# Late outputs through two matmul banks and a last chunk in three parts, a unit of filler work in every step, and the recurrence's banks marked at the start

## The chip, the cores and the metric

One NeuronCore of a Trainium2 chip runs the whole program in one launch. Time is device time in microseconds (us). The engines are named as in the profile: PE (TensorE, matmuls), PEld (its weight loads), DVE (VectorE), ACT (ScalarE), POOL (GpSimd), SP (SyncE, which issues most transfers). Before: a median of 1362.26 us in 3 runs (1359.16 to 1363.05).

## The reference

The input x has 8 sequences of 512 positions and 256 channels, and there is a conditioning vector per sequence. Four residual layers follow each other, all in float32:

- layer 0: a shared gated MLP plus 8 experts, of which each position uses 2;
- layer 1: a wavelet transform, gated and inverted; since the gate is constant along the sequence, the kernel multiplies by a factor instead;
- layer 2: a low-rank adapter whose weights are made from the conditioning vector;
- layer 3: a gated recurrence over the 512 positions, with one output product per position.

```python
def step(H, xs):
    xz, xr, xh = xs
    Z = jax.nn.sigmoid(xz + H @ Whz.T + bhz)
    R = jax.nn.sigmoid(xr + H @ Whr.T + bhr)
    H_tilda = jnp.tanh(xh + R * H @ Whh.T + bhh)
    H_new = Z * H + (1.0 - Z) * H_tilda
    Y = H_new @ Whq.T + bhq
    return (H_new, Y)
```

The result is x plus the four residuals. The recurrence is strictly serial; layers 0 to 2 work on each position alone, so a window of positions can be prepared while earlier positions run through the recurrence.

## The kernel before

The sequence is cut into 16 windows of 32 positions (256 columns with the batch) for layers 0 to 2, and into 32 chunks of 16 positions for the recurrence. The program has three stages.

*Prologue.* Loads, the conditioning products, the routing of the first four windows, the generated adapter weights and the first windows of layers 0 to 2. The prologue uses its own matmul (PSUM) banks: `c` for small products, `gp` for generated adapter weights, `more` as a third bank for the hidden products of window 0. When the prologue's pools are closed, these banks pass to the recurrence.

*The loop.* 512 steps are written out one after the other (from line 1262 on). A step is: r and z products of the state (PE, line 1113), sigmoid (ACT, 1279), transposes (DVE, 1293), r times state (1310), the candidate's product (PE), tanh (ACT), transpose, and a scan that makes the new state (DVE, 1367). Then ACT copies the state into the chunk's history `hist` (1381). Input products and biases for later steps are put into gate banks ahead of time: `grh` (two buffers, r and candidate) and `gz` (z, both halves in one bank). The biases are written there by ACT, and the input and state products accumulate onto them, so each bank has to be marked once beforehand by matmuls that write all of it: `claim` (lines 1143 to 1149, called just before the loop; 12 matmuls of 512 columns).

*Filler work.* All other work is cut into jobs, held in queues per engine. One PE unit is four matmuls side by side (`quads`, line 413). `Jobs.fill` takes ready jobs at fixed places of a step, by the planner's own clock (2.43 us per step): on PE an early slot between the z products and the candidate's product, and a late slot behind the candidate's product. Each slot is asked for a number of units: the early one for 1 and the late one for 2 when `behind(s)` says that more units are left than a straight line down to step 462 allows, and both for none otherwise (or for 1 each once the queue is empty, `late(s)`). Within an engine the emitted order is the order of execution.

*Outputs.* At the end of each chunk `output_jobs` queues its four PE units (two halves of the channels by two of the contraction), two DVE operations that add the product, the bias and x in place (line 1202), and, where a block of positions is complete, the transfers out on SP (line 1214). Chunks 0 to 11 go to the urgent queue; chunks 12 to 31 are held in `jobs.last`, which is opened when PE's other queues are empty. All of them use one bank, `r_m` ("misc"), which holds both channel halves; the next chunk takes it when both DVE operations are done. After the loop `jobs.drain` emits what is left.

Of the kernel before, what the change touches and what calls it, by code (L numbers as in the profile page):

```python
# [9 lines left out]
F32 = mybir.dt.float32  # L10
# [6 lines left out]
P = 128  # L17
# [16 lines left out]
GS = 4  # L34
NG = TC // GS
TO = 64
HELD = 12
EPS_GATE = 1e-09
EPS_LN = 1e-05
# [26 lines left out]
class Ring:  # L66

    def __init__(self, pool, tag, shape, bufs):  # L70
        self.pool, self.tag, self.shape = pool, tag, shape
        self.held = [None] * bufs
        self.made = self.asked = 0

# [8 lines left out]
    def take(self, lazy):  # L83
        self.held[self.made % len(self.held)] = lazy
        self.made += 1
        return self.pool.tile(
            self.shape, F32, name=f"{self.tag}_{self.made}", tag=self.tag
        )
# [108 lines left out]
def cond_resid_kernel(  # L197
# [76 lines left out]
    r_mid = ring("mid", pair, 2)  # L274
    r_xt = ring("xt", [P, KC, WS, B], 3)

    jobs = Jobs()

    def load(out, in_, mb, lazies=(), deps=()):
# [35 lines left out]
    def load_x(n, mb):  # L315
# [21 lines left out]


    r_w2 = Ring(pro.enter_context(tc.tile_pool(name="w2q", bufs=5)), "w2", [P, R * C], 5)
    r_c, r_gp, r_more = (  # L340
        Ring(pro.enter_context(tc.tile_pool(name=n, bufs=b, space=PSUM)), n, shape, b)
        for n, shape, b in (("c", [P, 512], 1), ("gp", [P, 512], 1), ("more", pair, 1))
    )
    pieces = {}
    for pair_ in LOW:
        for k in range(KC):
# [63 lines left out]
    def quads(out, lhs, rhs, start, tiles=NQ):  # L410

        for j in range(tiles):
            nc.tensor.matmul(  # L413
                out[ts(j, 32)],
                lhs[:, ts(j, 32)],
                rhs,
                start=start,
                stop=False,
                skip_group_check=True,
            )  # L420
# [4 lines left out]
    def window_jobs(w, routed, xt, via_pool=False):  # L425
# [57 lines left out]
        def bank():  # L483

            turn[0] += 1
            return Lazy(r_more if w == 0 and turn[0] % 3 == 0 else r_h)

        def hidden(lazy, n, lhs, got):
            last = None
# [499 lines left out]
    for n, of in enumerate(LOW):  # L989
        pick = set1.tile([P, 2, R, B], F32, name=f"pick{n}")  # L990
        nc.vector.memset(pick, 0.0)
        for side, q in enumerate(of):
# [3 lines left out]
                .rearrange("p (r o) -> p r o", o=1)  # L996
                .broadcast_to([4 * R, R, B]),
            )
        gp = Lazy(r_gp)

        def biased_rows(gp=gp, pick=pick):
            quads(gp.get()[:, :C], pick.rearrange("p s r b -> p (s r b)"), b2, True)

        j = pe(biased_rows, [got_b2], [gp], 0.45)
        for k in range(KC):
            got = [pieces[q, k] for q in of]

            def generate(k=k, of=of, gp=gp):
                for r in range(R // 2):
                    for t in range(NQ):  # L1010
                        w = pieces[of[t // 2], k][0].get()
                        nc.tensor.matmul(
                            gp.get()[ts(t, 32), :C],
                            hid[:, r, k, :],
                            w[:, ts(R // 2 * (t % 2) + r, C)],
                            start=False,
                            stop=False,
                            skip_group_check=True,
                        )

            j = pe(
                generate,
                [j, got_hid, *(g[1] for g in got)],
                [gp, *(g[0] for g in got)],
                1.75,
            )
        j = got_low_out[n] = dve(
            lambda n=n, gp=gp: nc.vector.tensor_copy(low_out[:, n], gp.get()[:, :C]),
            [j],
            [gp],  # L1030
            0.45,
# [43 lines left out]
    with (  # L1075
        tc.tile_pool(name="gw", bufs=1) as gw,
        tc.tile_pool(name="gs", bufs=3) as gs,
        tc.tile_pool(name="ps_g", bufs=2, space=PSUM) as ps_g,
        tc.tile_pool(name="ps_z", bufs=1, space=PSUM) as ps_z,
    ):  # L1080
        brow = brows[0]
        tt(brow, brow, brows[1], ALU.add)
# [9 lines left out]
        for u in range(GS):  # L1092
# [6 lines left out]
            s = gw.tile([P, KC, B, 2], F32, name=f"d0_{u}")  # L1099
            nc.vector.memset(s, 0.0)  # L1100
            d0s.append(s)


        gz = ps_z.tile([P, 2, NG, FQ], F32, name="gz")

        def new_gates(c):
            rh = ps_g.tile([P, NG, 2, FQ], F32, name=f"grh_{c}", tag="grh")
            return rh, gz[:, c % 2]

        def across(out, lhs, rhs, start=False):  # L1110

# [29 lines left out]
                lambda: bias(z, brow[:, 1]),  # L1141
            ]

        def claim(banks):

            some = wsq_a[:, 0, 0:2].rearrange("p a (n f) -> p a n f", f=FQ)
            for out in banks:
                for j in range(NQ):
                    nc.tensor.matmul(
                        out[ts(j, 32)], ident[:, 0:32], some, start=True, stop=True  # L1150
                    )

        def project(g, gates):

            rh, z = gates
# [17 lines left out]
        def state(u):  # L1173
            return lambda k: s_h[u][:, k, :, :, 1]

        last_out = {}

        def output_jobs(c, hist, copied):
            queue = jobs.urgent if c < HELD else jobs.last
            ps = Lazy(r_m)  # L1180
            last = None
            for m in range(KC):
                for k in range(KC):
                    last = jobs.add(
                        "PE",
                        lambda m=m, k=k: quads(
                            ps.get()[:, m, : TC * B],
                            wh[:, k, G_Q, ts(m, P)],
                            hist[:, k].rearrange("p t b -> p b t"),
                            k == 0,  # L1190
                        ),
                        [last, copied],
                        [ps],
                        0.45,
                        queue,
                    )
            t0 = c * TC
            at, tile_x = [g for g in xg if g[0] <= t0][-1]

            def finish(m):  # L1200
                x = tile_x[:, m, :, t0 - at : t0 - at + TC]
                stt(
                    x,
                    ps.get()[:, m, : TC * B].rearrange("p (b t) -> p b t", t=TC),
                    vec[:, V_HQ, m : m + 1],
                    x,
                    ALU.add,
                    ALU.add,
                )

                t1 = t0 + TC
                n = TO if t1 <= T - TO else 2 * TC if t1 == T - 2 * TC else TC
                if t1 % n == 0 and (n < TO or t1 % TO == 0) and t1 != T - 3 * TC:
                    nc.sync.dma_start(
                        out=outs_[:, m, :, t1 - n : t1],
                        in_=tile_x[:, m, :, t1 - n - at : t1 - at],
                    )

            for m in range(KC):
                last_out[c] = jobs.add(  # L1220
                    "DVE", lambda m=m: finish(m), [last], [ps], 0.3, queue
                )

        both = [new_gates(c) for c in range(2)]
        claim([gz] + [g[0].rearrange("p n g f -> p g n f") for g in both])
        gates = both[0]
        for part in biases(gates):
            part()
# [33 lines left out]
        for c in range(NTC):  # L1262
            hist = hists[c]
            gates = upcoming
            for t in range(TC):
# [64 lines left out]

                ahead = s + 5
                part = None
                if c + 1 < NTC and t == 6:
                    upcoming = new_gates(c + 1) if c else both[1]
                    bias_parts = biases(upcoming)
# [17 lines left out]
                cand, act_c = gate(rh[:, n, 1], AF.Tanh, "c", KC)  # L1353
                if part is not None:
                    part()
                jobs.fill("PE", now + 1.44, 2 if behind(s) else 1 if late(s) else 0)
                if bias_parts and t >= 7:
                    biased.append(bias_parts.pop(0)())
                    if not bias_parts:
# [24 lines left out]
                    last_copy.done = at + 0.2  # L1384

                last_copy = Job("ACT", None, [], [])
            output_jobs(c, hist, last_copy)
        copying(base)
        jobs.drain(base + T * STEP)

# [64 lines left out]
```

## Time and profile before

| what | us |
|---|---|
| median of the runs | 1362.26 |
| profiled execution | 1358.07 |
| its span, first to last instruction | 1355.9 |
| first scan of the loop starts at | 78.95 |
| last scan of the loop starts at | 1338.25 |
| PE busy, DVE busy, ACT busy | 1179.3, 913.8, 503.7 |

A row in order of time gives the start, the length, the engine, the line, the operation, the tiles written and read, and how many instructions were merged (each float32 matmul appears as two rows). In brackets stands the engine's idle time before the row and what ended it. A line for a stretch gives, for each engine, the busy time and the number of instructions, then the clock that was granted to PE (1.00 is full), the share of the DMA engines and their rate. PE's busy time counts each matmul from its start to its modelled end, and matmuls overlap, so it is no measure of how much more would fit.

### The profile page before, as it was taken

The numbers are of one execution on the slowest core, as the hardware profiler recorded it, in microseconds if no ns is written. First come the engines' busy times: TensorE is split into PE (matmuls) and PEld (weight loads), VectorE is DVE, ScalarE is ACT, GpSimd is POOL, SyncE is SP. The second block draws the span as 40 slices with busy tenths as digits, with TensorE's granted clock in tenths as the row PEclk, the third lists the DMA queues.
The fourth block names the chain that finished last, engine by engine and source line by source line (L and its number), as shares of the span: only waits on it lengthen the run. The fifth ranks groups of instructions, "written<-read, shape, count | busy, mean of one in ns | idle before, by whom it ended". The sixth has DMA issues, their size and how long they took to land.

```text
span 1355.9 us, 89216 instructions
## 1 busy us (share of the span) xinstructions
PE 1179.3 (87%) x39380; PEld 722.5 (53%) x39380; DVE 913.8 (67%) x6248; ACT 503.7 (37%) x3402; POOL 137.4 (10%) x203
## 2 busy tenths in 40 slices
PE   7999998989898998988898888888888888878776
PEld 4555555555555555555455555555555555545443
DVE  4267777776776767676676766667676767666664
ACT  1133334343343434334343433434343343433331
POOL 0211010101011110101011010101101010110000
PEclk8999999999999999999999999999999999999999
DMA  9631001100101010100101010010101000000102
GB/s 348 208 126 35 5 5 36 52 5 5 36 20 35 5 35 4 42 14 5 35 4 35 4 35 4 4 35 4 35 4 35 4 5 4 5 4 5 34 20 33
DMA packets 47092, 46.48 MB, mean 34 GB/s; under 512 B 24064, under 2 KB 44000, under 8 KB 45296
## 3 DMA queue, kind: packets, MB, share of 16 engines
q1 hardware_dynamic: 46384, 38.65, 9.3%
q8 instruction: 307, 5.03, 1.5%
q0 software_dynamic: 320, 2.13, 0.4%
q14 instruction: 81, 0.66, 0.2%
HBM read 36.45 MB, written 4.33 MB: 30 GB/s over the span
## 4 chain that ended last, share of the span: by engine, by line
PE 73%; DVE 14%; ACT 7%; issue 4%; DMA 2%; SPq 1%; DVEq 0%; ACTq 0%
PE grh L1113 33%; PE hp L413 13%; PE acc L413 10%; DVE rT L1293 6%; PE misc L413 6%; PE gz L1113 5%; PE low L413 4%; ACT r L1279 4%; DVE d L1293 3%; DVE s_rh L1310 2%; ACT c L1279 2%; DVE s_h L1367 2%; DMA x<-in_xT_dram 1%; SPq L283 1%; DMA wh<-in_sq_b_dram 1%
## 5 line engine op out<-in xcount | busy, mean ns | idle before, releaser
L1113 PE MATMUL grh<-wh,s_h 128*32 128x64 f32 x8192 | 227.5, 226 | 103.6 <-DVE s_h L1367 100.9
L1293 DVE STREAM_TRANSPOSE rT<-r 128x32 f32<-128x32 f32 x1024 | 156.0, 190 | 233.1 <-ACT r L1279 230.2
L1279 ACT ACTIVATE r<-grh 128x32 f32<-128x32 f32 x1024 | 146.2, 195 | 445.3 <-PE grh L1113 442.9
L1113 PEld LDWEIGHTS grh<-wh,s_h 128*32 128x32 f32 x8192 | 145.8, 110 | 256.1 <-DVE s_h L1367 251.2
L1113 PE MATMUL grh<-wh,s_rh 128*32 128x64 f32 x8192 | 224.4, 226 | 49.2 <-DVE s_rh L1310 25.2
L1279 ACT ACTIVATE c<-grh 128x32 f32<-128x32 f32 x1024 | 146.3, 195 | 315.4 <-PE grh L1113 313.2
L1113 PEld LDWEIGHTS grh<-wh,s_rh 128*32 128x32 f32 x8192 | 141.7, 109 | 202.9 <-DVE s_rh L1310 197.5
L1293 DVE STREAM_TRANSPOSE d<-c 128x32 f32<-128x32 f32 x1024 | 156.6, 192 | 121.0 <-ACT c L1279 114.8
L1113 PE MATMUL gz<-wh,s_h 128*32 128x64 f32 x8192 | 212.7, 220 | 1.3 <-issue 1.2
L1113 PEld LDWEIGHTS gz<-wh,s_h 128*32 128x32 f32 x8192 | 156.2, 111 | 1.7 <-issue 1.6
L413 PE MATMUL hp<-x,sw_sb 128*32 128x256 f32 x2016 | 152.3, 388 | 2.3 <-ACT sig L509 1.0
L413 PE MATMUL hp<-x,rw_sb 128*32 128x256 f32 x2016 | 151.8, 383 | 1.4 <-ACT sig L541 0.6
L557 POOL TENSOR_TENSOR g<-gl,bc 128x256 f32<-128x256 f32 x128 | 93.8, 733 | 532.3 <-DVE s_h L1367 348.9
L1367 DVE TENSOR_TENSOR_SCAN s_h<-d,d 128x16 f32<-128x16 f32 x1024 | 145.3, 184 | 0.0
L413 PE MATMUL acc<-g,rw_sb 128*32 128x256 f32 x2048 | 144.4, 379 | 0.1
L1310 DVE TENSOR_TENSOR s_rh<-rT,s_h 128x8 f32<-128x8 f32 x1024 | 133.7, 168 | 0.0
L1293 DVE STREAM_TRANSPOSE zT<-z 128x64 f32<-128x64 f32 x512 | 121.9, 238 | 1.1 <-ACT z L1279 1.0
L1279 ACT ACTIVATE z<-gz 128x64 f32<-128x64 f32 x512 | 121.1, 237 | 1.9 <-PE gz L1113 1.5
L1113 PE MATMUL grh<-wx,xt 128*32 128x128 f32 x2048 | 108.7, 275 | 2.2 <-ACT r L1279 2.2
L1381 ACT COPY hist<-s_h 128x16 f32<-128x16 f32 x512 | 106.1, 207 | 0.5 <-DVE s_h L1367 0.5
L1322 DVE TENSOR_TENSOR d<-zT,s_h 128x16 f32<-128x16 f32 x512 | 90.5, 177 | 17.5
L1323 DVE TENSOR_SCALAR d<-zT 128x16 f32<-128x16 f32 x512 | 86.6, 169 | 0.0
(146 smaller groups left out, 1202.8 us busy)
## 6 DMA issues: line engine op xcount, KB each, us to landing
bc<-comb_d SPq DMA_DIRECT2D x56, 256.0 KB, 4.1
w<-in_w_dram SPq DMA_DIRECT2D x8, 1024.0 KB, 17.2
out_dram<-x SPq DMA_DIRECT2D x14, 256.0 KB, 3.1
x<-in_xT_dram SPq DMA_DIRECT2D x2, 1536.0 KB, 9.7
rw_sb<-in_rw_dram SPq DMA_DIRECT2D x2, 1024.0 KB, 13.3
bc<-comb_d POOLq DMA_DIRECT2D x2, 1024.0 KB, 10.8
sw_sb<-in_sw_dram SPq DMA_DIRECT2D x3, 512.0 KB, 5.5
wsq_a<-in_sq_a_dram SPq DMA_DIRECT2D x1, 1280.0 KB, 9.7
```

The costliest lines, as they stand in the source:

```text
L283: lambda: nc.sync.dma_start(out=out.get() if isinstance(out, Lazy) else out, in_=in_),
L413: nc.tensor.matmul(out[ts(j, 32)], lhs[:, ts(j, 32)], rhs, start=start, stop=False, skip_group_check=True,)
L557: lambda gl=gl, g=g, e=e: nc.gpsimd.tensor_tensor(g.get().rearrange("p (h t) -> p h t", t=P), gl.get().rearrange("p (h t) -> p h t", t=P), ...
L1113: nc.tensor.matmul(out[ts(j, 32)], lhs, rhs[:, ..., ts(j, FQ)], start=start, stop=False, skip_group_check=True,)
L1279: nc.scalar.activation(x, y, func)
L1293: ins = nc.vector.transpose(dst.rearrange("p i u b -> p i (u b)"), src.rearrange("p (i r) -> p i r", r=32),)
L1310: prod = tt(s_rh[u][:, k, u, :], rT[:, k, u, :], h[:, k], ALU.mult)
L1322: tt(d1[:, :, u, :, 1], zT[:, :, u, :], h, ALU.mult)
L1323: nc.vector.tensor_scalar(d0[:, :, :, 1], zT[:, :, u, :], -1.0, 1.0, ALU.mult, ALU.add)
L1367: new = nc.vector.tensor_tensor_scan(s_h[v][:, k, v].rearrange("p b w -> p (b w)"), d0[:, k].rearrange("p b w -> p (b w)"), d1[:, k, u].re ...
L1381: nc.scalar.copy(hist[:, :, t, :], s_h[v][:, :, v, :, 1])
```

## The change

- Held outputs (chunks 12 to 31) no longer use the one bank `r_m`: each channel half takes one of the two buffers of `r_h`, the banks of the hidden products, and each half's DVE operation depends on its own half alone.
- The last chunk's output is queued in three parts: its first 8 positions at step 7 of the chunk, the next 4 at step 11, the last 4 (`TAIL`) after the loop. Its very last transfer is issued by ACT instead of SP.
- The late slot is asked for 2 units when behind and for 1 otherwise, in every step.
- The gate banks are allocated at the outset. `gz` and the first `grh` buffer are marked before anything else on PE, by 8 matmuls of 256 columns each over a tile of zeros; the second `grh` buffer serves the prologue's small products (instead of `c`) and is marked in step 4 of the loop. `gp` and `more` are gone: the generated weights use `r_m`, and window 0's third bank is `r_low`.

```diff
+TAIL = 4
...
     def take(self, lazy):
         self.held[self.made % len(self.held)] = lazy
         self.made += 1
+        if self.given is not None:
+            return self.given
...
+    ps_g = pool_of("ps_g", 2, PSUM)
+    ps_z = pool_of("ps_z", 1, PSUM)
+    gz = ps_z.tile([P, 2, NG, FQ], F32, name="gz")
...
+    both = [new_gates(c) for c in range(2)]
+    zeros = const.tile([P, NT], F32, name="zeros")
+    nc.vector.memset(zeros, 0.0)
+    rh0, rh1 = [g[0].rearrange("p n g f -> p (n g f)") for g in both]
+
+    def claim(bank):
+
+        for half in range(2):
+            for j in range(NQ):
+                nc.tensor.matmul(
+                    bank[ts(j, 32), ts(half, NT)],
+                    zeros[:, 0:32],
+                    zeros,
+                    start=half == 0,
+                    stop=half == 1,
+                    skip_group_check=True,
+                )
+
+    claim(gz.rearrange("p c n f -> p (c n f)"))
+    claim(rh0)
...
+    r_c = Ring(None, "c", None, 1, rh1)
...
-            return Lazy(r_more if w == 0 and turn[0] % 3 == 0 else r_h)
+            return Lazy(r_low if w == 0 and turn[0] % 3 == 0 else r_h)
...
-        gp = Lazy(r_gp)
+        gp = Lazy(r_m)
...
-        def output_jobs(c, hist, copied):
-            queue = jobs.urgent if c < HELD else jobs.last
-            ps = Lazy(r_m)
-            last = None
+        def output_jobs(c, hist, copied, a=0, n=TC):
+
+            held = c >= HELD
+            queue = jobs.last if held else jobs.urgent
...
+                t1 = t0 + a + n
+                size = TO if t1 <= T - TO else 2 * TC if t1 == T - 2 * TC else TC
+                if t1 % size or (size < TO and t1 == T - 3 * TC):
+                    return
+                (nc.scalar if t1 == T and m else nc.sync).dma_start(
+                    out=outs_[:, m, :, t1 - size : t1],
+                    in_=tile_x[:, m, :, t1 - size - at : t1 - at],
+                )
+
+            ps = None if held else Lazy(r_m)
+            todo, last = [], None
             for m in range(KC):
+                if held:
+                    ps = Lazy(r_h)
+                half = 0 if held else m
...
+                    [j if held else last],
...
-        claim([gz] + [g[0].rearrange("p n g f -> p g n f") for g in both])
...
+                if c == 0 and t == 4:
+                    claim(rh1)
...
-                jobs.fill("PE", now + 1.44, 2 if behind(s) else 1 if late(s) else 0)
+                jobs.fill("PE", now + 1.44, 2 if behind(s) else 1)
...
-            output_jobs(c, hist, last_copy)
+                if c == NTC - 1 and t in (TC // 2 - 1, TC - TAIL - 1):
+                    a = 0 if t < TC // 2 else TC // 2
+                    output_jobs(c, hist, last_copy, a, t + 1 - a)
+            if c < NTC - 1:
+                output_jobs(c, hist, last_copy)
+        output_jobs(c, hist, last_copy, TC - TAIL, TAIL)
         copying(base)
         jobs.drain(base + T * STEP)
```

## The prediction

> **What bounds the kernel now.** I read the page first (span, chain), then the rows in order of time for the last 30 us, then stretches of the 512 steps, and last the first 76 us.
>
> ```profile
> span 1355.9 us, 89216 instructions
> PE 73%; DVE 14%; ACT 7%; issue 4%; DMA 2%; SPq 1%; DVEq 0%; ACTq 0%
> out_dram<-x SPq DMA_DIRECT2D x4, 64.0 KB, 2.5
> ```
>
> The chain is mostly PE, but it is a loop through PE, ACT and DVE. Rows in order of time show what one turn costs:
>
> ```profile
> 1328.58 0.28 DVE L1367 TENSOR_TENSOR_SCAN s_h<-d,d 128x16 f32<-128x16 f32 x2
> 1330.27 1.11 PE L413 MATMUL misc<-hist,wh 128*32 128x128 f32 x16
> 1331.00 0.28 DVE L1367 TENSOR_TENSOR_SCAN s_h<-d,d 128x16 f32<-128x16 f32 x2
> 1331.72 0.64 PE L413 MATMUL misc<-hist,wh 128*32 128x128 f32 x8
> 1332.69 0.65 PE L413 MATMUL misc<-hist,wh 128*32 128x128 f32 x8
> 1333.42 0.28 DVE L1367 TENSOR_TENSOR_SCAN s_h<-d,d 128x16 f32<-128x16 f32 x2
> 1335.83 0.28 DVE L1367 TENSOR_TENSOR_SCAN s_h<-d,d 128x16 f32<-128x16 f32 x2
> ```
>
> The columns are start, length, engine, line. One block unit is 8 matmul rows. Two units in the late slot (after the candidate's matmuls), one in each slot, and none at all: the scans stay 2.42 us apart. So the step is the loop's latency, and units cost nothing where they fit. From the first scan (78.95) to the last (1338.25) 511 steps take 1259.3 us; at 2.42 they would take 1236.6. The 22.7 us between are stalls. Of these 7.5 are waits of PE for nothing but issue (the waits of PE between 76 and 1339, "issue" rows added: 4.2 + 1.2 + 1.0 + 0.7 + 0.4). Another part is the clock:
>
> ```profile
> 513.10:516.52 3.42, 1.81 (x80) 1.21 (x80) 2.50 (x18) 1.88 (x11) 0.00 (x0) 1.00 0.02 5
> 516.52:519.93 3.41, 2.89 (x84) 2.39 (x88) 2.69 (x17) 0.90 (x7) 0.00 (x0) 0.50 0.02 7
> 516.45 0.28 DVE L1367 TENSOR_TENSOR_SCAN s_h<-d,d 128x16 f32<-128x16 f32 x2
> 519.32 0.28 DVE L1367 TENSOR_TENSOR_SCAN s_h<-d,d 128x16 f32<-128x16 f32 x2
> ```
>
> In the first two lines PE's busy time is the second number, the granted clock the last but two. After a stretch in which PE was busy 1.81 of 3.42 us the next 3.41 us ran at 0.50, and the steps in it took 2.87 and 2.63 instead of 2.42 (scans at 516.45, 519.32, 521.95): 0.66 lost. There are seven such stretches (from 352.68, 427.77, 516.52, 595.03, 752.04, 987.56, 1233.32); the steps in them lost 1.2, 1.0, 0.7, 1.0, 1.1, 1.2 and 0.5, together 6.7.
>
> The end:
>
> ```profile
> 1338.25 0.29 DVE L1367 TENSOR_TENSOR_SCAN s_h<-d,d 128x16 f32<-128x16 f32 x2
> 1339.64 0.61 DVE L1202 SCALAR_TENSOR_TENSOR x<-misc,vec,x 128x128 f32<-128x128 f32 x2 [1.10 <-PE misc L413]
> 1340.39 2.04 PE L413 MATMUL misc<-hist,wh 128*32 128x128 f32 x32 [0.82 <-DVE x L1202]
> 1351.19 0.61 DVE L1202 SCALAR_TENSOR_TENSOR x<-misc,vec,x 128x128 f32<-128x128 f32 x2 [2.26 <-PE misc L413]
> ```
>
> After the last scan five chunks' outputs go through one bank, 2.87 us each (matmuls, DVE, wait), and the span ends 17.4 us behind that scan (1338.54 to 1355.9). Last, the start of the loop:
>
> ```profile
> 2.56 0.99 PE L881 MATMUL c<-cond,inv_c 128*128 128x8 f32 x4 [2.56 <-DVE pick L991]
> 8.76 1.79 PE L763 MATMUL c<-rout,x 128*32 128x8 f32 x120 [1.30 <-DMA x<-in_xT_dram]
> 66.66 2.28 PE L1149 MATMUL grh<-wsq_a,ident 128*32 128x512 f32 x16
> 67.14 0.36 DVE L1082 TENSOR_TENSOR brow<-brow,brow 128x192 f32<-128x192 f32 x1 [0.99 <-DMA brow<-in_bias_rows_dram]
> 68.38 2.08 PE L413 MATMUL low<-mid,wsq_a 128*32 128x256 f32 x30
> 68.74 0.41 DVE L615 TENSOR_TENSOR u<-misc,own 64x256 f32<-64x256 f32 x1
> 70.32 1.00 PE L413 MATMUL low<-u,low_out 128*32 128x256 f32 x12
> ```
>
> **The change part by part**, priced against the profiled execution (1358.07 us, 2.2 of it around the span).
>
> *Tail.* The order as built has 80 output matmuls (20 units) behind the last step before, 16 narrow ones (4 units of 32 columns) after; from step 466 to 505 nearly every step now carries two. They fit: steps with two late units kept 2.42 above, and the one DVE finish per step (0.33) lies in DVE's 0.69 us between a scan's end and the next transpose (1328.86 to 1329.55). What remains behind the last scan: the history copy 0.03 + 0.21; four units, between 0.4 (31 matmuls of 8 columns took 0.44) and 2.05 (32 matmuls of 128 columns), I take 0.6, because with a quarter of the columns they lie nearer to the narrow row; two finishes between 0.17 and 0.33 each, 0.4; 2.5 from issue to landing of 64 KB; 1.2 from the last landing to the end, as now (issued 1352.2 + 2.5 = 1354.7, end 1355.9). With 0.1 for two handovers that is 5.0: **-12.4**. The second half's transfer is issued by ACT, which issues none before. Bounds: as SP's (2.5), and POOL's 5.1 to landing for 32 KB. Best case 4.6 (-12.8), worst 9.0 (-8.4).
>
> *Marks at the outset.* 16 matmuls of 256 columns (four units) now head PE's queue, behind a memset of 128x256 (0.28 on DVE). At the rates of that time (1.06 per unit at 10.38, 0.67 mean over the 64 rows from 11.21) they take 2.7 to 4.2 and end near 3.9 to 5.3; the conditioning matmul behind them started at 2.56. That chain ran 4.6 us (2.56 to 7.16) to the first router products, so it reaches them at 8.5 to 9.9. The bulk of the products waited until 8.76 for x anyway, so the loss is 0 to 1.1 there; PE is nearly full from then to 76, and the delay is carried. I take **+0.5**, range -0.5 to +1.5, since the clock stood at 0.50 from 21.6 to 35.2 and may fall otherwise.
>
> *Marks at 66 us gone.* PE is relieved of 2.4 us (65.95 to 68.38). What is late next: `low<-u` waits for u, which stands on DVE behind brow, and brow waited for its own DMA until 67.14. So u is still ready at 69.15, while `low<-u` began at 70.10: **-0.9**, between 0 and -2.4.
>
> *Mark of the third bank in step 4.* Two units more in the early slot. Without a unit PE idles there 0.54 us (z's matmuls end at 1329.48, the candidate's start at 1330.02); one unit (0.43) is already in it. So 0.1 of 0.86 is hidden: **+0.75**, 0.3 to 0.9.
>
> *One unit in every step.* In the built order the steps whose late slot is empty fall from 130 to 32, those without any unit from 34 to 23. Price of the 98 filled slots: 0, since the late slot holds two units (0.86) at 2.42; without that cover 0.43 each, 42 us. The total of units is the same. Gain: fewer stretches of over 3.4 us without a unit, 30 before, 16 after. All seven half-clock stretches follow one of the 30. Measured by the length above 3.4, there is room for 12.4 clock windows before and 8.3 after, so 4.7 drops are left of 7: 2.3 x 0.95 = **-2.0**, between 0 and -6.7. The gaps that stay are where no unit is ready: around steps 334 and 366 they even grow.
>
> The Trainium skill ("TensorE: Matmul & The Clock Gate", Part 1: The HAM clock gate) says the clock halves after an idle window of about 3.4 us that runs free of the program. The trace agrees on the 3.41 us and differs on idle: PE was busy 1.81 us in the stretch before the drop. By the page's rule no step here is idle that long, this part would be worth nothing, and the sum would be two microseconds smaller.
>
> *The rest.* Buffers renamed in the prologue (`gp` to misc, `more` to low) keep PE's order; their previous readers are long done, 0. Issue waits stay at 7.5, +-3, because the transfers they meet are the same.
>
> Sum: -12.4 + 0.5 - 0.9 + 0.75 - 2.0 = **-14.05**, so 1344.0 for an execution like the profiled one. The median of the runs lies 4.2 above it (1362.26), so the forecast is 1362.26 - 14.05 = **1348.2**.
>
> **The rivals.**
> 1. *Slower or equal:* the newly filled late slots hold units whose input is late. The next step's r matmuls stand behind them in PE's queue, and ACT and DVE wait for those. 98 slots: from 0.14 us each (14.05 / 98) it eats the gain; at one DVE operation each (0.4) it ends at 1348.2 + 39 = 1387. Against it: 381 steps filled that slot before, and the waits of PE show one wait of a unit for DVE (0.4 us).
> 2. *The clock no longer drops at all:* -6.7 instead of -2.0: 1343.5. For it: any unit lifts a stretch; against it, 16 gaps remain.
> 3. *The change does not do all it says:* the last part's matmuls run like today's 2.05 and ACT's transfer like POOL's 5.1: tail 9.0, time 1352.2.
>
> **How the numbers follow.** Chances: forecast 0.70, rival 1 0.07, rival 2 0.14, rival 3 0.09. A measurement here can tell about 0.3% (4 us) from no change. Only rival 1 brings less than that gain: 0.03 within, 0.04 slower; faster 0.93. The range takes the forecast's bounds (best -12.8 - 0.5 - 2.4 + 0.3 - 6.7 = -22, worst -8.4 + 1.5 + 0 + 0.9 + 0 = -6), not all at once, and the spread of the runs shown (-3, +1): 1342 to 1356.5.
>
> **What would show it.** Tail: under 6 us from last scan to end, four short units, one output transfer from ACT. Steps: 2.42 between scans in steps 240 to 330 with one or two units; a period of 2.5 there is rival 1. Clock: three to six half-clock stretches behind step 0. Step 4: longer by about 0.75. First scan: 78.5 instead of 78.95. The prediction is wrong if the loop's 511 steps take over 1262 us, or the tail over 9.

## The result, and the profile after

| | before | after |
|---|---|---|
| median of 6 runs each, same chip, us | 1358.65 | 1345.85 |
| lowest to highest, us | 1355.55 to 1363.05 | 1343.38 to 1351.22 |
| ratio, 95% interval | | 0.9907 [0.9878, 0.9935] |
| profiled execution, us | 1358.07 | 1344.15 |
| its span, us | 1355.9 | 1342.3 |

The change saves 12.8 us. A second set of 6 runs of the changed kernel, against 14 of before, gave 1346.05 and 0.99 [0.9872, 0.9929]. The forecast was 1348.2. Only part of that agreement is merit: two errors of opposite sign leave a miss of 2.35. The sum said -14.05 and 12.8 were gained, which is 1.25 less; the base was 3.6 too high, since 1362.26 was the median of three runs and six put it at 1358.65.

The page of after, span and chain by engine. PE's share has fallen (73% before), DVE's risen (14%), and waits for issue stand at 5% (4%):

```profile
span 1342.3 us, 89396 instructions
PE 68%; DVE 17%; ACT 8%; issue 5%; DMA 1%; SPq 1%; DVEq 0%; ACTq 0%
```

So the time has to be split by stage. I cut the span at the end of the first scan and at the end of the last one (read from the scan rows in order of time). "Stalls" is what the 511 steps took over 511 x 2.418. "Issue" is the part of them in which PE waited for nothing that the profile shows. "Half clock" is how long the granted clock stood at 0.50, up to the end of the first scan and from there to the end of the last.

| profiled execution | first scan ends | 511 steps | stalls (issue) | tail | half clock before / in the loop |
|---|---|---|---|---|---|
| before | 79.24 | 1259.30 | 23.7 (7.0) | 17.32 | 13.7 / 23.9 |
| after | 74.83 | 1262.14 | 26.5 (14.7) | 5.37 | 10.2 / 14.0 |
| after, second profile | 73.29 | 1264.59 | 29.0 (12.0) | 5.38 | 3.4 / 31.9 |

The tail gave 11.95, the start gave 4.4 (5.95 in the second profile), and the loop took 2.8 back (5.3 in the second).

**Tail.** After, rows in order of time (start, length, engine, line, operation). Five chunks in one bank, 2.87 us each, stood here before:

```profile
1336.68 0.28 DVE L1390 TENSOR_TENSOR_SCAN s_h<-d,d 128x16 f32<-128x16 f32 x2
1337.00 0.20 ACT L1404 COPY hist<-s_h 128x16 f32<-128x16 f32 x1 [0.51 <-DVE s_h L1390]
1337.26 0.71 PE L443 MATMUL hp<-hist,wh 128*32 128x32 f32 x32 [1.12 <-ACT hist L1404]
1337.78 0.49 DVE L1197 SCALAR_TENSOR_TENSOR x<-hp,vec,x 128x32 f32<-128x32 f32 x2 [0.81 <-PE hp L443]
1338.06 0.53 SPq L1210 DMA_DIRECT2D out_dram<-x  x1
1338.31 0.64 ACTq L1210 DMA_DIRECT2D out_dram<-x  x1
```

After, the transfers of the last 8 us (size, median us from issue to landing):

```profile
out_dram<-x SPq DMA_DIRECT2D x1, 64.0 KB, 2.5
out_dram<-x ACTq DMA_DIRECT2D x1, 64.0 KB, 2.9
```

One chunk's last quarter is left: a copy, four narrow units in 0.71, two finishes in 0.49, two transfers. The one from ACT lands 2.93 behind its issue (at 1341.24), and the span ends 1.09 later.

**Where the other chunks went.** After, rows in order of time, some 50 us ahead of the last scan. Rows of the recurrence's own products are left out. Each late slot holds two output units (16 rows), each step one finish, and the scans come after 2.41 and 2.47 us:

```profile
1285.73 1.11 PE L443 MATMUL hp<-hist,wh 128*32 128x128 f32 x16
1286.46 0.28 DVE L1390 TENSOR_TENSOR_SCAN s_h<-d,d 128x16 f32<-128x16 f32 x2
1286.66 0.33 DVE L1197 SCALAR_TENSOR_TENSOR x<-hp,vec,x 128x128 f32<-128x128 f32 x1
1288.26 1.11 PE L443 MATMUL hp<-hist,wh 128*32 128x128 f32 x16
1288.87 0.29 DVE L1390 TENSOR_TENSOR_SCAN s_h<-d,d 128x16 f32<-128x16 f32 x2
1289.08 0.33 DVE L1197 SCALAR_TENSOR_TENSOR x<-hp,vec,x 128x128 f32<-128x128 f32 x1
1290.61 1.11 PE L443 MATMUL hp<-hist,wh 128*32 128x128 f32 x16
1291.34 0.28 DVE L1390 TENSOR_TENSOR_SCAN s_h<-d,d 128x16 f32<-128x16 f32 x2
```

**Clock.** After, stretches of one clock window each (PE's busy time is the second number, the granted clock the last but two):

```profile
903.04:906.45 3.41, 1.76 (x88) 1.17 (x80) 2.76 (x18) 1.84 (x12) 0.00 (x0) 1.00 0.02 5
906.45:909.87 3.42, 3.42 (x72) 2.39 (x68) 1.98 (x14) 0.89 (x6) 0.00 (x0) 0.51 0.01 2
1322.99:1326.40 3.41, 1.74 (x80) 1.26 (x80) 1.96 (x16) 0.99 (x9) 0.00 (x0) 1.00 0.00 0
1326.40:1329.81 3.41, 2.12 (x76) 1.84 (x80) 1.97 (x16) 1.18 (x9) 0.00 (x0) 0.50 0.03 7
1329.81:1333.22 3.41, 2.39 (x72) 1.83 (x72) 2.08 (x15) 0.89 (x6) 0.00 (x0) 0.50 0.00 0
302.40:305.81 3.41, 1.69 (x89) 1.21 (x92) 1.42 (x12) 0.40 (x3) 0.00 (x0) 1.00 0.02 5
305.81:309.23 3.42, 2.71 (x104) 1.79 (x98) 1.75 (x12) 0.93 (x7) 0.00 (x0) 1.00 0.02 5
```

The pattern of before is there again: a window with PE busy 1.7 to 1.8 us, then one at half clock. The last two lines show that this is no threshold: behind a window with 1.69 us the clock stayed at 1.00. What is new is the place. The held outputs are now finished by step 505, the last parts cannot start before their steps, and of the six steps behind 505 only two (508 and 509) carry units. The clock falls at 1326.40 and stays down to the end. Steps 508 to 511 take 0.22, 0.45, 0.44 and 0.45 longer, 1.56 in all. Before, where the backlog filled the end, the last six steps lost 0.01. So 1.6 of the tail's gain is given back in the steps ahead of it.

**Start and step 4.** After, rows in order of time:

```profile
1.20 1.94 PE L298 MATMUL gz<-zeros 128*32 128x256 f32 x16 [1.20 <-DVE zeros L291]
2.90 1.93 PE L298 MATMUL grh<-zeros 128*32 128x256 f32 x16
4.77 0.92 PE L911 MATMUL grh<-cond,inv_c 128*128 128x8 f32 x4
8.91 1.79 PE L793 MATMUL grh<-rout,x 128*32 128x8 f32 x120 [0.31 <-DMA x<-in_xT_dram]
64.33 0.36 DVE L1110 TENSOR_TENSOR brow<-brow,brow 128x192 f32<-128x192 f32 x1 [1.10 <-DMA brow<-in_bias_rows_dram]
66.39 1.07 PE L443 MATMUL low<-u,low_out 128*32 128x256 f32 x16 [1.22 <-DVE u L645]
82.60 0.28 DVE L1390 TENSOR_TENSOR_SCAN s_h<-d,d 128x16 f32<-128x16 f32 x2
83.36 1.05 PE L298 MATMUL grh<-zeros 128*32 128x256 f32 x16
85.60 0.28 DVE L1390 TENSOR_TENSOR_SCAN s_h<-d,d 128x16 f32<-128x16 f32 x2
```

The marks push the conditioning matmul from 2.56 to 4.77, but the router products, which wait for x, only from 8.76 to 8.91. Where the old marks stood, PE now waits 1.22 us for `u`, and `u` stands behind `brow` and its DMA. The mark in step 4 makes that step 3.00 long, 0.58 more than 2.42.

**Issue waits.** After, waits of PE between 76 and 1338 us (reader's line, total us, count, largest):

```profile
PE misc L793 <- issue: 5.4, 5, 1.8
PE gz L1134 <- issue: 4.3, 5, 1.3
PE grh L1134 <- issue: 4.1, 6, 1.1
PE hp L443 <- issue: 1.0, 1, 1.0
```

Together 14.8, where before had 7.5 (from the first scan on 14.7 and 7.0). The first row is the router's products, long rows of matmuls of 8 columns, in steps 27 to 29, 59 to 61 and 91. Of the rest, most lie two or three steps behind a burst of four loads of `bc` (256 KB each) on SP: steps 16, 76, 139, 169, 201, 265, 297, 393.

### The profile page after: what moved, and what is told of

It reads as the page before. It is cut to its first block, busy times and chain, and to the rows that moved or that the text cites. A ratio compares the mean times of both kernels' runs of the same rounds, so it can differ in the third digit from the quotient of the medians.

```text
span 1342.3 us, 89396 instructions
## 1 busy us (share of the span) xinstructions
PE 1176.8 (88%) x39468; PEld 706.5 (53%) x39468; DVE 913.2 (68%) x6253; ACT 504.5 (38%) x3402; POOL 137.3 (10%) x203
## 3 DMA queue, kind: packets, MB, share of 16 engines
q8 instruction: 308, 5.05, 1.5%
## 4 chain that ended last, share of the span: by engine, by line
PE 68%; DVE 17%; ACT 8%; issue 5%; DMA 1%; SPq 1%; DVEq 0%; ACTq 0%
PE grh L1134 33%; PE hp L443 14%; PE acc L443 7%; DVE rT L1314 6%; PE gz L1134 5%; DVE d L1314 5%; PE low L443 5%; ACT r L1300 4%; PE misc L443 3%; ACT c L1300 3%; DVE s_rh L1331 2%; DVE s_h L1390 2%; SPq L316 1%; DMA wh<-in_sq_b_dram 1%; DMA x<-in_xT_dram 0%
## 5 line engine op out<-in xcount | busy, mean ns | idle before, releaser
L1134 PE MATMUL grh<-wh,s_h 128*32 128x64 f32 x8192 | 223.3, 226 | 78.6 <-DVE s_h L1390 76.3
L443 PE MATMUL acc<-g,rw_sb 128*32 128x256 f32 x2048 | 148.9, 379 | 0.0
## 6 DMA issues: line engine op xcount, KB each, us to landing
rw_sb<-in_rw_dram SPq DMA_DIRECT2D x2, 1024.0 KB, 13.3
```

The costliest lines, as they stand in the source:

```text
L443: nc.tensor.matmul(out[ts(j, 32)], lhs[:, ts(j, 32)], rhs, start=start, stop=False, skip_group_check=True,)
L1134: nc.tensor.matmul(out[ts(j, 32)], lhs, rhs[:, ..., ts(j, FQ)], start=start, stop=False, skip_group_check=True,)
```

## The experiments

Theory: nearly all of the gain is the output part (two banks instead of one), and the other parts are worth little. The rivals: the start's 4.4 us are the marks', or the unit in every step is worth several microseconds. Each ratio is against before on the same chip; the sections ran on different chips, so between sections the ratios are compared.

### The output part alone

Before, with the new `output_jobs` and its calls and nothing else:

```diff
+                if held:
+                    ps = Lazy(r_h)
+                half = 0 if held else m
...
+                if c == NTC - 1 and t in (TC // 2 - 1, TC - TAIL - 1):
+                    a = 0 if t < TC // 2 else TC // 2
+                    output_jobs(c, hist, last_copy, a, t + 1 - a)
```

> Only the output part of the change: held outputs through two banks, the last chunk in three parts. My theory: the 12 us at the end come from this part alone. From last scan to end about 5.4 us (17.3 before), the rest as before, 12 us faster, 1346.5 against 1358.5. Rival: without a unit in every step the held units do not get through in time and some are left for the end: tail 8 us or more, at most 9 us faster.

Measured: 1343.61 us, ratio 0.9902 [0.9879, 0.9924]. Tail 5.37, first scan 74.57 without any half clock in the prologue, 511 steps 1259.66 with issue waits of 7.3. This part alone brings all that the whole change brings.

### A unit in every step alone

```diff
-                jobs.fill("PE", now + 1.44, 2 if behind(s) else 1 if late(s) else 0)
+                jobs.fill("PE", now + 1.44, 2 if behind(s) else 1)
```

> Only the late slot's request changed (one unit where none was asked for). My theory: fewer half-clock stretches between first and last scan (2 to 5, seven before), waits of PE for nothing but issue unchanged by it (7 to 15 us, by chance of the execution), tail 17.3: 2 us faster, hardly to be told from no change. Rival: units moved forward into the bursts of transfers make the issue waits longer by the 7 us seen in the changed kernel's trace: 0 to 5 us slower.

Measured: 1358.67 us in 12 runs against 1357.86 in 23, ratio 0.9999 [0.9982, 1.0015], that is -2.4 to +2.0 us. The forecast's -2.0 lies inside, and so does nothing at all. Its profile has five half-clock stretches in the loop, seven before. In it 44 late slots stay empty, 130 before; 86 more filled slots that cost even 0.05 us each would have shown (4.3 us), which speaks against the first rival of the prediction. The steps without any unit do not fall, though: 35 here, 34 before, and 22 in the output part alone. The stretches of over 3.4 us without a unit go the same way: 31 before, 30 here, 17 with the output part alone, 16 after, and 30 again in after with one bank (below). It is the second bank that takes these gaps away, not this rule.

### The marks alone

```diff
+    claim(gz.rearrange("p c n f -> p (c n f)"))
+    claim(rh0)
...
-        claim([gz] + [g[0].rearrange("p n g f -> p g n f") for g in both])
...
+                if c == 0 and t == 4:
+                    claim(rh1)
```

> Only the banks marked at the outset, with the third bank's mark in step 4. Theory of the prediction: first scan ends 0.4 us earlier, step 4 is 0.6 us longer: no change. Rival, from the changed kernel's trace, where the first scan ended 4.4 us earlier: the marks wake PE's clock, and the half-clock stretch of the prologue (13.7 us before) is shorter by about 7 us in each execution: first scan 4 us earlier, 3.5 us faster.

Measured: 1357.55 us, ratio 1.0002 [0.998, 1.0024]. First scan at 74.31, and no half clock in the prologue. The kernel with the output part alone, which has the old marks, also ran its prologue at full clock and reached 74.57. So between these two profiles the marks bring the first scan forward by 0.26, not by 4.4, and even that is not shown: the ten profiles of kernels with the marks, whose prologues are the same, spread from 73.29 to 75.56. The rest of the 4.4 lies in the execution that was profiled of before: 13.7 us at half clock from 21.6 us on. At 20.6 us its products were 0.8 us behind those of the output part alone, at 36.1 us 7.0. A kernel without new marks (the unit in every step alone) started at 76.49, with 3.4 us at half clock at 39.3, while after with 10.2 us, most of them at 22.5, lost only 0.5 against the marks alone: what a window costs in the prologue depends on where it falls. Step 4 cost 0.58 here too, and 0.03 in before.

### One bank for the held outputs

After, but the held outputs use `r_m` again, and the three parts and all else stay:

```diff
-            ps = None if held else Lazy(r_m)
+            ps = Lazy(r_m)
...
-                if held:
-                    ps = Lazy(r_h)
-                half = 0 if held else m
+                half = m
```

> The changed kernel, the last chunk still in three parts, but the held outputs through one bank with both halves, as before. My theory: the two banks are what lets the held units through in the steps; with one, four chunks or so are left behind the last step, at 2.9 us each: tail 14 to 17 us, time 1355. Rival: the unit asked for in every step carries them through one bank as well: tail 5.4, 1346.

Measured: 1360.15 us, ratio 1.0017 [0.9997, 1.0038]; tail 18.93, both more than the theory allowed. The whole gain is gone. Rows in order of time of this kernel, behind its last scan at 1340.35:

```profile
1341.71 0.61 DVE L1197 SCALAR_TENSOR_TENSOR x<-misc,vec,x 128x128 f32<-128x128 f32 x2 [1.08 <-PE misc L443]
1342.46 2.08 PE L443 MATMUL misc<-hist,wh 128*32 128x128 f32 x32 [0.81 <-DVE x L1197]
1344.59 0.61 DVE L1197 SCALAR_TENSOR_TENSOR x<-misc,vec,x 128x128 f32<-128x128 f32 x2 [2.27 <-PE misc L443]
1352.97 0.69 PE L443 MATMUL misc<-hist,wh 128*32 128x32 f32 x32 [0.69 <-DVE x L1197]
1354.27 0.69 PE L443 MATMUL misc<-hist,wh 128*32 128x32 f32 x32 [0.61 <-DVE x L1197]
```

The chunks go one by one through `misc` again, each waiting for the finish of the one ahead of it, and the last chunk takes three turns where one would do. In the loop it is the same: around 1290 us this kernel fits four units into three steps (two behind the candidate at 1288.42, one early and one late in the next, none behind the candidate at 1293.30), where after fits two into each. Allowing more units per step does not help while a chunk waits for its bank. The second bank is what lets the slots be used; the three parts and the unit in every step bring nothing without it.

### The last chunk in one part

```diff
-                if c == NTC - 1 and t in (TC // 2 - 1, TC - TAIL - 1):
-                    a = 0 if t < TC // 2 else TC // 2
-                    output_jobs(c, hist, last_copy, a, t + 1 - a)
-            if c < NTC - 1:
-                output_jobs(c, hist, last_copy)
-        output_jobs(c, hist, last_copy, TC - TAIL, TAIL)
+            output_jobs(c, hist, last_copy)
```

> The changed kernel with the last chunk's output in one part behind the last step, still through two banks. The tail then has four units of 128 columns (2.05 us in the kernel before), two finishes of 0.33 and both transfers: 6.9 us instead of 5.4, so the three parts are worth 1.5 us and the two banks the other 10.5. Rival: without the parts the chunk also finds the banks taken, tail 8 or more.

Measured: 1349.96 us, 0.9931 [0.9902, 0.9959], against 0.99 [0.9872, 0.9929] of the changed kernel on the same chip. The intervals overlap, so the difference in time (3.9) is not settled by the runs. The tail's rows are clearer. This kernel, in order of time, last scan ending at 1343.55, end at 1350.0:

```profile
1343.84 2.08 PE L443 MATMUL hp<-hist,wh 128*32 128x128 f32 x32 [1.20 <-ACT hist L1404]
1345.98 0.35 DVE L1197 SCALAR_TENSOR_TENSOR x<-hp,vec,x 128x128 f32<-128x128 f32 x1 [0.58 <-PE hp L443]
1346.36 0.65 ACTq L1210 DMA_DIRECT2D out_dram<-x  x1
```

Four full units take 2.08 in place of 0.71, and the tail is 6.45 in place of 5.37: the three parts are worth 1.1 of the tail's 12. The last six steps lost 2.6 at half clock here (1.56 in after), where still less work is left for them.

### The issue waits: loads spread out

The 511 steps were longer than the prediction allowed, and the issue waits had doubled. Theory: PE waits for its own instructions while bursts of loads are under way. Test: after, but each load of `bc` in the loop waits for the scan of the step before, so that the four no longer come at once (`fetch` returns its DMA):

```diff
+        def pace(made):
+            if new is not None and made is not None:
+                after(made, new)
...
-                jobs.fill("SP", now, 1)
+                jobs.fill("SP", now, 1, then=pace)
```

> The changed kernel, but each of the four loads of bc per window waits for the scan of the step in which it is emitted, so that they start one per step and not four in 1.5 us. Theory of the burst: the issue waits of PE (14.8 us in the changed kernel's trace) come from instruction fetches queued behind the four loads; they fall below 5 us: 8 us faster than the changed kernel, 1338. Rival: they come from the fetch itself, whatever else is on the transfer engines: 12 to 15 us again, 1346. A third: the loads arrive too late and POOL's products with them: new waits on g, 1350 or more.

Measured: 1340.45 us, 0.9867 [0.9845, 0.9889]. This kernel's waits of PE between 76 and 1340 us:

```profile
PE misc L793 <- issue: 6.9, 5, 2.5
PE low L443 <- issue: 0.3, 1, 0.3
```

14.8 fell to 7.2, less than the theory wanted (below 5). Gone is every wait behind step 92, where after had 6.3 us in seven; up to there 7.2 are left of 8.4, and the router's row among them has grown. The next pair of kernels shows the same. So the waits behind step 92 came from the bursts. Those in the steps of the router's products have another cause, which no run here finds. The worth in time is less sure: 5.4 us under the median of after, with intervals that just touch.

The same pacing on the kernel with the output part alone:

> The output part alone, with the loads of bc paced one per step; neither marks at the outset nor a unit in every step. If the other two parts are worth nothing, as their own runs said: as fast as the changed kernel with paced loads, 1340. Rival: with paced loads out of the way the unit in every step shows its 2 us: 1342 or more. Issue waits of PE 4 to 8 us.

Measured: 1345.33 us, 0.9879 [0.9847, 0.9912]; without pacing it was 1343.61, 0.9902 [0.9879, 0.9924], and the changed kernel with paced loads had 0.9867. The time is the rival's (1342 or more), but all three intervals overlap: no difference is shown, neither by the pacing nor by the other two parts. The issue waits there were only 7.3 to begin with, and 6.0 paced: behind step 92 they fell from 2.5 to none, and up to there they stayed (4.8 and 6.0, of which 2.9 stand at the recurrence's `grh`). In this profile the clock was down for 45.1 us of the loop, against 28.5 without pacing.

The changed kernel unaltered, on the same chip as that run, as a measure of how much a profile of one kernel varies:

> The changed kernel once more, for a second trace beside the experiments. If the issue waits of PE in its first trace (14.7 us against 7.0 before) belong to the change, they are 13 to 16 us again; if they are chance, they fall between 7 and 11 us as in the three runs of the parts, and the loop's steps take 1256 to 1261 us instead of 1262. The first scan ends at 74.3 to 76.5 in either case, tail 5.4, time 1345.

Measured: 1346.05 us. The tail is the same to 0.01 us; half clock in the loop 31.9 us in place of 14.0; issue waits 12.0 in place of 14.7, between the two forecasts; the first scan ended at 73.29, earlier than expected. Issue waits in all profiles without the marks at the outset and not paced: 7.0, 7.3, 9.1. With the marks: 14.7, 12.0, 13.2, 11.7, 10.3 (and 8.8 with the zeros of the next section). Part of it lies at the router's products: in steps 27 to 30, 59 to 62 and 91 to 92 the first three have 3.4 to 3.6 us, the five with the marks 5.3 to 6.5. Why a kernel with them has more is open. That the stream of instructions meets the loads at other places would do it, but no run here shows it.

### Keeping the clock up

Of the 24.7 us of stalls in the paced kernel's profile 7.2 are issue waits, and the clock stood at half for 36.9 us of its loop. If windows without units are what drops it, then units of no use should hold it. Paced kernel, and wherever the late slot gets no unit, PE multiplies zeros onto the z bank, which adds nothing to it:

```diff
-                jobs.fill("PE", now + 1.44, 2 if behind(s) else 1)
+                if not jobs.fill("PE", now + 1.44, 2 if behind(s) else 1):
+                    for _ in range(4):
+                        across(z[:, n], zeros[:, 0:32], zeros)
```

> The changed kernel with paced loads, and in each of the 32 steps whose late slot stays empty 16 matmuls of 64 columns of zeros into the z bank, which change nothing in it. My theory: half-clock stretches come from stretches of over 3.4 us without a unit, and those are gone: 0 or 1 half-clock stretch in the loop (8 in the paced kernel's trace), 4 to 6 us less, 1335. Rival: products of zeros or of 64 columns do not keep the clock up, or the drops have another cause: 4 or more stretches, 1340.

Measured: 1336.87 us, 0.9825 [0.9793, 0.9856]; the mean granted clock of its runs 0.995 (0.985 without the zeros). Half clock in the loop: one window of 3.4 us, where the paced kernel had 36.9. The last six steps lose nothing. The stalls fell from 24.7 to 19.9, and 14.0 of these lie in the first 96 steps. The same without pacing:

> The changed kernel, loads of bc not paced, with the products of zeros in the 32 empty late slots. My theory: the clock and the bursts are separate losses: 0 to 2 half-clock stretches in the loop, granted clock 0.99 or more, issue waits 12 to 15 us as in the changed kernel, 3.5 us faster than it, 1342. Rival: part of the issue waits are the slow clock's, and they fall too: 1338.

Measured: 1338.07 us, 0.9838 [0.9812, 0.9864], clock 0.996, and 6.8 us at half clock. Against the changed kernel's 1345.85 and 1346.05 this is 8 us less, and the intervals of the ratios lie apart. The theory missed (1342, issue waits of 12 to 15), and the rival's number came true: the issue waits of this profile are 8.8, against 14.7 and 12.0. So the products of zeros are worth 8 us; how much of that is the clock itself and how much the issue waits that fell with it is not separated. Pacing on top adds 1.2, which the intervals do not separate from nothing.

With zeros, is the unit in every step still of use? Paced, zeros, and the old rule for the late slot:

```diff
-                if not jobs.fill("PE", now + 1.44, 2 if behind(s) else 1):
+                if not jobs.fill("PE", now + 1.44, 2 if behind(s) else 1 if late(s) else 0):
```

> The changed kernel with paced loads and products of zeros, but the late slot asked for units by the rule of before (none where PE is neither behind nor out of work), so that the products of zeros fill many more late slots. My theory: a unit in every step was worth only what it did for the clock, so with the clock held by other means the rule is worth nothing: 1337, as with the new rule. Rival: the even spread of units saves waits by itself: 1340 or more.

Measured: 1345.11 us, 0.9902 [0.9873, 0.9931], though the clock held at 0.994. That is 8 us over the same kernel with the new rule. Rows of this kernel's waits of PE:

```profile
PE gz L1134 <- issue: 5.0, 9, 1.1
PE grh L1134 <- issue: 4.7, 7, 1.0
PE misc L793 <- issue: 3.7, 2, 2.8
PE hp L443 <- issue: 0.6, 2, 0.3
```

Issue waits of 14.0 are back, although the loads are paced. Its steps lose 6.0 more than with the new rule, and its issue waits are 6.6 more. The old rule leaves 119 slots empty in place of 33, and each gets 16 products. This kernel's group of zeros (rows x count | busy us, mean ns | idle before):

```profile
L1134 PE MATMUL gz<-zeros 128*32 128x64 f32 x3808 | 78.3, 219 | 3.1 <-issue 3.0
```

Two causes were open, the number of instructions or the old rule itself. The same columns of zeros in a quarter of the instructions tell them apart:

```diff
-                    for _ in range(4):
-                        across(z[:, n], zeros[:, 0:32], zeros)
+                    for j in range(NQ):
+                        nc.tensor.matmul(
+                            z[ts(j, 32)],
+                            zeros[:, 0:32],
+                            zeros,
...
```

> The kernel with paced loads, zeros in the empty late slots and the old rule for the late slot again, but each empty slot gets 4 products of 256 columns of zeros in place of 16 of 64: the same columns in a quarter of the instructions (238 empty slots: 952 instructions, not 3808). Theory A (the 1345.11 us of the kernel with 16 came from PE's instruction stream: its 20 waits for nothing but issue took 14.0 us, against 7.4 with the new rule, and nine of them ahead of the z matmuls and the products of zeros): the issue waits fall to 7 to 9 us, the 511 steps to 1255 to 1258, the time to 1337 to 1341. Theory B (it came from the old rule itself, that is from where the units lie): issue waits and time stay, 12 to 15 us and 1343 to 1347. Theory C (4 products of zeros are too little to hold the clock, as they keep PE's parts busy for a shorter time): half-clock stretches come back, four or more, at 0.9 to 1.0 us each, and the time lies at 1341 to 1346 with issue waits under 9.

(The 238 slots in that text are 119: each product of the code stands as two rows in the profile. The counts of rows are right.) Measured: 1335.31 us, 0.9818 [0.9767, 0.9868], clock 0.996. The group of zeros and the waits of this kernel:

```profile
L1387 PE MATMUL gz<-zeros 128*32 128x256 f32 x952 | 74.1, 379 | 0.0
```

```profile
PE grh L1134 <- issue: 2.3, 2, 1.4
PE misc L793 <- issue: 2.0, 3, 1.4
PE hp L443 <- issue: 1.6, 1, 1.6
PE gz L1134 <- issue: 0.2, 1, 0.2
```

PE is busy with zeros for about as long (74.1 and 78.3 us), the rule is the same, and 10 us are gone. Issue waits fell from 14.0 to 6.1 and the steps' stalls from 25.9 to 14.8; both lie below what the first theory expected. So it was the form of the zeros, a quarter of the instructions for the same columns, and the many cost more than their issue waits alone. Half clock did not come back (one window). This version is the fastest profile of all (1332.6 us); its interval and that of 1336.87 overlap, and both beat both kernels of the case.

## Why the prediction was right, and where it was wrong

*Tail, -12.4: right, -11.95.* The rows from the last scan to ACT's issue took 1.34, as summed. Of the rest, the landing was mis-sized: 2.93 for ACT's transfer, where 2.5 was taken from SP's row, and 1.09 instead of 1.2 to the end. The 2.93 is not ACT's own figure: with the last chunk in one part ACT issued 0.93 us behind SP, not 0.25, and its 64 KB landed after 2.54. The bound from POOL's transfer (5.1) was not needed. That a finish per step and two units in the late slot fit beside a step of 2.42 held: the 20 units that had stood behind the loop left no trace in the steps from 466 to 505. Missed was what this does to the end of the loop: with the backlog gone, four of the last six steps have no units, the clock drops, and 1.56 to 1.77 us are lost there in after, its second profile and the output part alone. Net, the output part gives 10.2 to 10.4 in the profiles; the runs of it alone give 13.3 [10.3, 16.4].

*Marks at the outset, +0.5, and marks at 66 us gone, -0.9: not refuted, -0.4 forecast, -0.26 between two prologues at full clock, less than such prologues vary.* `brow`'s DMA does hold `u`, as the step said. The first scan at 74.83 instead of the 78.5 that it named is clock: the sum had been made against an execution with 13.7 us at half clock and kept that as if it belonged to the kernel.

*Step 4, +0.75: 0.58.* The cover was mis-sized: of 0.86 not 0.1 but 0.28 is hidden.

*One unit in every step, -2.0 (0 to -6.7): not refuted, not shown, and credited to the wrong part.* Alone it gives -2.4 to +2.0. (The step's own product, 2.3 x 0.95, is 2.2.) Its premise was that the rule takes the stretches without a unit from 30 to 16. The kernel as a whole has 16, but the rule alone leaves 30, after with one bank has 30, and the output part alone gives 17. The mean granted clock of the rule's 12 runs is 0.986 against 0.984 for before, one or two windows less and within the scatter of the runs; that of the output part alone is 0.984 too. Single profiles with the new rule and without zeros had 14 to 44 us at half clock in the loop, so the few windows of after say little. The prediction read seven windows off one profile as if their number were steady.

*Issue waits stay at 7.5, +-3, "because the transfers they meet are the same": wrong.* They were 14.7 and 12.0. The transfers are the same, and the reason is not enough: with the same loads spread out the waits behind step 92 go and the others stay, and 3808 rows of zeros bring waits back that 952 do not. Why the changed kernel has more is open. In the first profile the rise in waits (7.7) is more than all of the loop's loss, as half clock was 9.9 us shorter there; in the second the waits are 4.9 more and half clock 8.0 longer. So the 511 steps took 1262.14 and 1264.59, past the 1262 that the prediction itself had set as its mark of failure. By that mark the loop's part of the forecast (-1.25 with step 4) failed: it was +2.8 in the profiled pair. In the profiled pair the sum survived (-13.9) because the start gave 4.0 us more than it had counted, and that was the half clock in before's prologue, not the change: luck.

*The clock's rule.* The windows at 903.04 and 1322.99 had PE busy 1.76 and 1.74 us of 3.41 and were followed by half clock. The Trainium skill ("TensorE: Matmul & The Clock Gate", Part 1: The HAM clock gate) has the clock halve after an idle window of about 3.4 us that runs free of the program. The window's length agrees with the 3.41 us here. Its word "idle" does not, since no window was. The runs with zeros show that too little activity is what counts: filling only the slots that were empty took the loop from 36.9 us at half clock to 3.4. How little is too little, PE's busy time does not tell: behind 302.40, with 1.69 us, the clock held.

*The rivals.* The first (late inputs hold the filled slots) fell with the run of that part alone. The second (the clock never drops) did not happen by the change; the zeros brought nearly that, and 8 us, more than the 4.7 between its time and the forecast. The third (tail 9.0) is refuted by the tail of 5.4.

## What to carry to other kernels

Work that is left over at the end is often held back not by the engine but by the one buffer it must pass through: look who frees the bank before allowing more work per slot, since more slots with one bank gave nothing, and the second bank, with all else equal, took the tail from 18.9 to 5.4 us and 14 us off the time. When a backlog is used up, ask what kept the clock up: products of zeros in the empty slots were worth another 8 us; in many slots they have to be few and wide. And a stretch at half clock or a wait for issue that one profile shows is a draw from a spread; price it from several executions before subtracting it.

## What the runs showed of the hardware

- The clock fell to half behind windows of 3.41 us in which PE was busy for about half of the time: 1.74 to 1.81 us in the lines shown. It did not always fall: after 1.69 us at 302.40 it held. Filling the slots with matmuls of zeros raised the mean granted clock from 0.985 to 0.995: products that change nothing count as activity.
- PE's waits for issue change with the number of instructions and with the other transfers. 3808 rows of 64 columns of zeros against 952 rows of 256, nearly the same busy time, made 14.0 and 6.1 us of waits. Spreading four loads of 256 KB over four steps removed the waits behind step 92 in two kernels without zeros (6.3 us to none, 2.5 to none) and left those before it. The profile lists transfers of kind "instruction" on a queue of its own, 308 packets and 5.05 MB in after, 338 and 5.54 MB with 3808 rows of zeros; that these are what PE waits for is likely, but no run shows it.
- A transfer of 64 KB issued by ACT landed after 2.9 us where SP had issued one 0.25 us earlier, which took 2.5 (3.4 and 3.2 in the kernel with wide zeros). Issued 0.93 us behind SP's, in the kernel with the last chunk in one part, ACT's took 2.54.
